# A graph network layer on one core: the residual of its output added by the store's DMA

## The chip, the cores and the metric

The kernel runs on one core of a Trainium2 chip. The metric is the device time of one execution in microseconds (us), the lower the better. It is given as the median of several executions; the profile is of one further execution.

## What is computed

The layer takes x, 32 graphs (batches) of 512 nodes with 256 features, and adj, their 512 x 512 adjacency matrices of zeros and ones, all in 32-bit floats. Cut to what matters:

```python
h = max(layernorm(x), 0)
conv  = relu(bn2(conv17(relu(bn1(conv1(h))))) + h)       # along the nodes
s     = h @ w_se.T + b_se
A     = exp(-|s_n - s_m|^2) * adj
nmp   = A @ relu(h @ w_msg.T + b_msg)
gi, gh = [conv, nmp] @ w_ih.T + b_ih,  h @ w_hh.T + b_hh
r, z  = sigmoid(gi_r + gh_r), sigmoid(gi_z + gh_z)
n     = tanh(gi_n + r * gh_n)
out   = x + (1 - z) * n + z * h
```

The change concerns the `x +` of the last line.

## The kernel before

**Layout.** Most of the work is done turned: features on the 128 partitions (two halves, `o` = 0 and 1), the 512 nodes of one batch along the free dimension. The result of one batch and one half is called an output block here: a tile of 128 x 512. There are 64 of them. The output in DRAM has nodes as rows, so a block has to be turned. VectorE's transpose turns pieces of 32 x 32, and the DMA places the pieces: `OB` and `XB` are views of the output and of x whose rows are nodes in 16 groups of 32. One block is moved by four DMAs of 64 KB, one for each group of 32 partitions, in pieces of 128 bytes (32 floats) in DRAM.

**Streams and plan.** The program is one long straight line of instructions without a loop on the chip. A planner written out in Python orders it when it is built. It keeps a clock `now` for TensorE and, for VectorE and ScalarE, the time at which each will be free (`dve.free`, `act.free`), from a cost for each instruction. Five streams take turns by due times: rows (first convolution), begins (layer norm and turning), graphs (messages and adjacency), conv (the 17 taps, as products in a transformed form), gates (what makes the output). `later(t, f)` puts work off to time t of the plan, and background work (sums, operands, weights) is added whenever VectorE's planned work ends soon. So a VectorE instruction more or less changes the places of later ones on all engines.

**Queues.** SP issues the loads in program order: weights `w` (L571), hidden rows `hT`, `hTg`, `hTb` (L211, L218, L225), `xconv` (L232), `xnb` (L252), adjacency (L340), turned inputs and residuals (`blocks`, L958). GpSimd (POOL) issues the stores: `hd` (L170, L993), `nd` (L170), `cd` (L721), `wd` (L583), `xd` (L979) and the output (L1140). Each of these instructions waits in its queue until its data or buffer is ready, and those behind it wait too. Several of the loads read what one of the stores wrote to DRAM.

**The output.** `gates(b)` runs over both halves. `reset` (L1151) and `update` (L1181) make the two gates on ScalarE, `mix_next` (L1095) the tanh, and then VectorE works off a block: in `mix_last` (L1102) `o_sb<-hTb,r`, `o_sb<-z,o_sb` and `r<-o_sb,r`, in `leave` (L1117) the transpose `o_sb<-r` and the addition `res<-o_sb,res`. `store` (L1136) writes `res` out with four DMAs on POOL. `load_res` (L963) loads the block of x, in the same turned-piece form, into one of two `res` buffers; `store` calls it for the block two later as soon as its own DMAs are issued, so these loads wait on SP for the store to free the buffer. The very last block (batch 31, half 1; `is_last`) is handled in two pieces along the nodes, with `mix_ahead` (L1126) doing what doesn't need the tanh earlier, and with its stores on the SP and ScalarE queues.

Of the kernel before, what the change touches and what calls it, by code (L numbers as in the profile page):

```python
# [8 lines left out]
F32 = mybir.dt.float32  # L9
AF = mybir.ActivationFunctionType  # L10
ALU = mybir.AluOpType
PSUM = bass.MemoryType.PSUM

P = 128
# [18 lines left out]
U = 29  # L33
Q = 18
# [15 lines left out]
def kernel(  # L50
# [31 lines left out]
    nc = tc.nc  # L82
    B, N, D = x.shape
# [19 lines left out]
    late = None  # L103
# [27 lines left out]
    dve, act = Engine(nc.vector, 0.12, 0.00108), Engine(nc.scalar, 0.16, 0.0009)  # L131

    def matmul(ps, lhsT, rhs, **more):
        nonlocal now
        now += max(0.223, 0.005 + elements(ps) / 600.0)
        nc.tensor.matmul(ps, lhsT, rhs, **more)  # L136
# [21 lines left out]
    def later(t, f):  # L158
        LATER.append((t, f))
        LATER.sort(key=lambda e: e[0])  # L160

    def settle():
        while LATER:
            LATER.pop(0)[1]()
# [14 lines left out]
    def settle_stores():  # L179
        while STORES:  # L180
            STORES.pop(0)()


    XS, HT, HB, HR, HR_AT, HG, XN, XR = {}, {}, {}, {}, {}, {}, {}, {}
# [35 lines left out]
    def load_gates(b):  # L220
        if b >= B or b in HB:
            return
        settle_stores()
        HB[b] = late.tile([P, ND, N], F32, name="hTb", bufs=2)
        nc.sync.dma_start(HB[b], HD[b])  # L225
        HB_AT[b] = now + 8.0
# [21 lines left out]
    def load_sums(b, d):  # L248
        if b < B and (b, d) not in XN:
            settle_stores()  # L250
            XN[b, d] = late.tile([P, N], F32, name="xnb", bufs=2)
            nc.sync.dma_start(XN[b, d], ND_[b, d])  # L252
# [700 lines left out]
    OB = out.rearrange("b (k i) d -> b i k d", i=32)  # L953

    def blocks(t, rows, o):
        for g in range(P // 32):
            at = o * P + 32 * g
            nc.sync.dma_start(  # L958
                t[32 * g : 32 * g + 32, :].rearrange("i (k j) -> i k j", j=32),
                rows[:, :, at : at + 32],  # L960
            )

    def load_res(b, o):  # L963
        if b < B and (b, o) not in XR:
            XR[b, o] = late.tile([P, N], F32, name="res", bufs=2)
            blocks(XR[b, o], XB[b], o)


# [91 lines left out]
    def gates(b):  # L1060

        nonlocal gating
        load_gates(b)
        gating = b
        load_sums(b, 0)
        load_sums(b, 1)
        if b == 0:
# [32 lines left out]
            later(act.free + 0.3, lambda: mix_last(r, z, o, s))  # L1100

        def mix_last(r, z, o, s):  # L1102
            load_res(b, o)
            y = XR[b, o]
            if is_last(o):
                dve.tensor_tensor(z[:, s], z[:, s], r[:, s], op=ALU.mult)
                dve.transpose(r[:, s], z[:, s])
                dve.tensor_tensor(y[:, s], r[:, s], y[:, s], op=ALU.add)
                later(dve.free + 0.4, lambda: store(y, o, s))
                return  # L1110
            t = late.tile([P, N], F32, name="o_sb")
            dve.tensor_tensor(t, hT[:, o, :], r, op=ALU.subtract)
            dve.scalar_tensor_tensor(t, z, 1.0, t, op0=ALU.add, op1=ALU.mult)
            dve.scalar_tensor_tensor(r, t, 0.5, r, op0=ALU.mult, op1=ALU.add)
            later(dve.free, lambda: leave(r, t, y, o))

        def leave(r, t, y, o):  # L1117

            dve.transpose(t, r)
            dve.tensor_tensor(y, t, y, op=ALU.add)  # L1120
            later(dve.free + 0.4, lambda: store(y, o, slice(0, N)))

        def is_last(o):
            return b == B - 1 and o == ND - 1
# [11 lines left out]
        def store(y, o, s):  # L1136
            for g in range(P // 32):
                at = slice(32 * g, 32 * g + 32)
                queue = nc.gpsimd if s.stop - s.start == N else nc.scalar if g % 2 else nc.sync
                queue.dma_start(  # L1140
                    OB[b][:, s.start // 32 : s.stop // 32, o * P + 32 * g : o * P + 32 * g + 32],
                    y[at, s].rearrange("i (k j) -> i k j", j=32),
                )
            if s.stop == N:
                del XR[b, o]
                load_res(b + o, 1 - o)

        for o in range(ND):
            r = z = None

            def reset():  # L1151
                nonlocal r
                settle()
                if b == 0:
                    load_res(b, o)
                r = late.tile([P, N], F32, name="r", bufs=2)
                act.activation(r, ps_r, AF.Tanh, bias=brz[:, o : o + 1], scale=0.5)

            def hidden_half(ps_h, s=slice(0, N)):
                act.activation(  # L1160
                    ps_h[:, s], ps_h[:, s], AF.Identity, bias=bn[:, o : o + 1], scale=0.5
                )

            halves = []

            hidden_at = 0.0

            def reset_hidden():
                nonlocal hidden_at
                while halves:  # L1170
                    ps, s = halves.pop(0)
                    dve.scalar_tensor_tensor(
                        ps[:, s], r[:, s], 1.0, ps[:, s], op0=ALU.add, op1=ALU.mult
                    )
                    hidden_at = dve.free + 0.3

            def reset_later(ps_h, s=slice(0, N)):
                halves.append((ps_h, s))
                later(act.free + 0.3, reset_hidden)

            def update():  # L1181
                nonlocal z
                z = late.tile([P, N], F32, name="z")
                act.activation(
                    z, ps_z, AF.Tanh, bias=brz[:, ND + o : ND + o + 1], scale=0.5
                )

            def mix(ps_n, s=slice(0, N)):
                later(now + 0.3, lambda r=r, z=z, o=o: mix_next(r, ps_n, z, o, s))

            ps_r = acc.tile([P, N], F32, name="ps_acc")
            ps_h = None
            yield from products(ps_r, o, 0, (0,), of=(0, 2))
            if o == 0:
                ps_h = acc.tile([P, N], F32, name="ps_acc")
                yield from products(ps_h, o, 2, (0,), lambda: hidden_half(ps_h))
                yield lambda: RES.get(b, 1e9) < 1e9
                yield RES[b]
                x_in.extend([XC[b][:, i, :] for i in range(ND)] + [XN[b, d] for d in range(ND)])
            yield from products(ps_r, o, 0, (1, 2), reset, (0, 2))  # L1200

            if ps_h is None and not is_last(o):
                ps_h = acc.tile([P, N], F32, name="ps_acc")
                yield from products(ps_h, o, 2, (0,), lambda: hidden_half(ps_h))
            if ps_h is not None:
                reset_later(ps_h)
            else:
                parts = []
                for s in (slice(0, N - P), slice(N - P, N)):
                    ps = acc.tile([P, N], F32, name="ps_acc")  # L1210
                    parts.append((ps, s))
                    for i in range(ND):
                        matmul(
                            ps[:, s], whh[:, i, cols(o, 2)], hT[:, i, s],
                            start=(i == 0), stop=(i == ND - 1), skip_group_check=True,
                        )
                    hidden_half(ps, s)
                    reset_later(ps, s)
                    yield now
            ps_z = acc.tile([P, N], F32, name="ps_acc")  # L1220
            yield from products(ps_z, o, 1, (0, 1, 2), update)
            if o == 0:
                load_gates(b + 1)
            if not is_last(o):
                reset_hidden()
                yield hidden_at
                yield from products(
                    ps_h, o, 2, (1, 2) if o == 0 else (2, 1), lambda: mix(ps_h), clear=False
                )
                continue  # L1230

            later(act.free + 0.2, lambda: mix_ahead(z, o))
            for ps, s in parts:
                for j in range(2 * ND):
                    matmul(
                        ps[:, s], wih[:, j, cols(o, 2)], x_in[j][:, s],
                        start=False, stop=(j == 2 * ND - 1), skip_group_check=True,
                    )
                mix(ps, s)
                yield now  # L1240
            settle()
# [109 lines left out]
    while 0 in NORMS:  # L1351
# [8 lines left out]
        op=ALU.add,  # L1360
# [10 lines left out]
    for b in (2, 3):  # L1371
        at = (b - 2) * NT * D
# [10 lines left out]
    while streams:  # L1383
# [10 lines left out]
        name = min(able, key=lambda k: clock[k])  # L1394
# [64 lines left out]
```

## Time and profile before

| | |
|---|---|
| median of 3 executions | 2083.01 us (2079.53 to 2084.8) |
| the profiled execution, and its span | 2089.1 us, 2087.2 us |
| first and last residual addition on VectorE | 303.9 us, 2082.7 us |
| loads of res on SP | 256 of 64 KB, median 4.1 us from issue to landing |
| stores of res on POOL | 252 of 64 KB, 649 ns each at the median, 2.8 us to landing |
| DMA packets | 545,861, of which 456,512 are under 512 bytes |
| HBM read and written | 278.55 MB and 98.04 MB |

The span runs from the first to the last instruction of the program in the profiled execution. Busy times of an engine are unions of its instructions. A group line gives the source line, the engine, the operation, what it writes and reads, and the count. A wait line gives the waiting engine and instruction, what released it, the sum in us, how many waits there were, and the longest. L127, L136 and L141 are lines of helpers through which nearly all VectorE, ScalarE and TensorE work is recorded, so groups are told apart by their tiles.

### The profile page before, as it was taken

The numbers are of one execution on the slowest core, as the hardware profiler recorded it, in microseconds if no ns is written. First come the engines' busy times: TensorE is split into PE (matmuls) and PEld (weight loads), VectorE is DVE, ScalarE is ACT, GpSimd is POOL, SyncE is SP. The second block draws the span as 40 slices with busy tenths as digits, with TensorE's granted clock in tenths as the row PEclk, the third lists the DMA queues.
The fourth block names the chain that finished last, engine by engine and source line by source line (L and its number), as shares of the span: only waits on it lengthen the run. The fifth ranks groups of instructions, "written<-read, shape, count | busy, mean of one in ns | idle before, by whom it ended". The sixth has DMA issues, their size and how long they took to land.

```text
span 2087.2 us, 25989 instructions
## 1 busy us (share of the span) xinstructions
PE 2053.2 (98%) x8724; PEld 1260.0 (60%) x8724; DVE 1364.5 (65%) x2441; ACT 827.7 (40%) x1585; POOL 337.4 (16%) x578
## 2 busy tenths in 40 slices
PE   9999999999999999999999999999999999999998
PEld 5888566666566565665666665456655666644444
DVE  6789677866778566875677764577774668643223
ACT  5544653333633346234353343533333533332221
POOL 2100121221211112111121111311110210021111
PEclk9999999999999999999999999999999999999999
DMA  7455778777877767786678775778674666434342
GB/s 281 151 176 187 237 227 220 200 197 203 238 193 206 205 174 214 201 212 160 188 220 216 187 193 155 197 188 222 177 202 145 185 175 163 145 95 106 73 96 41
DMA packets 545861, 378.36 MB, mean 181 GB/s; under 512 B 456512, under 2 KB 473440, under 8 KB 545088
## 3 DMA queue, kind: packets, MB, share of 16 engines
q1 hardware_dynamic: 512848, 278.76, 50.8%
q0 software_dynamic: 28192, 84.70, 12.6%
q10 hardware_dynamic: 4688, 13.24, 1.7%
q8 instruction: 70, 1.15, 0.2%
q14 instruction: 63, 0.52, 0.1%
HBM read 278.55 MB, written 98.04 MB: 180 GB/s over the span
## 4 chain that ended last, share of the span: by engine, by line
PE 93%; DVE 3%; ACT 2%; DMA 1%; issue 1%; POOL 0%; SPq 0%; ACTq 0%; DVEq 0%
PE ps_acc L136 47%; PE ps_c L136 22%; PE ps_g L136 21%; PE ps_g L141 1%; PE ps_c L917 1%; DVE z L127 1%; DMA xconv<-cd 0%; PE ps_acc L146 0%; DVE st L127 0%; ACT h L127 0%; PE ps_g L917 0%; DVE x L127 0%; ACT y L127 0%; ACT x_sb L127 0%; DVE at L127 0%
## 5 line engine op out<-in xcount | busy, mean ns | idle before, releaser
L136 PE MATMUL ps_acc<-xconv,wih 128*128 128x512 f32 (+1 forms) x772 | 365.0, 595 | 0.0
L136 PE MATMUL ps_acc<-xnb,wih 128*128 128x512 f32 (+1 forms) x772 | 360.2, 592 | 0.0
L136 PE MATMUL ps_acc<-hTb,whh 128*128 128x512 f32 (+1 forms) x772 | 356.0, 590 | 0.0
L136 PEld LDWEIGHTS ps_c<-xd,w 128*128 128x128 f32 x2304 | 289.0, 191 | 64.2 <-issue 58.6
L136 PEld LDWEIGHTS ps_c<-x,w 128*128 128x128 f32 x2032 | 258.2, 192 | 89.8 <-issue 64.6
L136 PE MATMUL ps_c<-xd,w 128*128 128x135 f32 (+1 forms) x2304 | 291.5, 279 | 0.2
L136 PE MATMUL ps_c<-x,w 128*128 128x135 f32 (+2 forms) x2032 | 268.0, 281 | 11.0 <-ACT z L127 4.4
L1140 POOL DMA_DIRECT2D out_dram<-res x252 | 164.1, 657 | 704.5 <-DVE res L127 580.8
L136 PEld LDWEIGHTS ps_acc<-xconv,wih 128*128 128x128 f32 x772 | 142.5, 192 | 146.3 <-issue 143.7
L136 PE MATMUL ps_g<-at,msg 128*128 128x512 f32 x512 | 227.6, 593 | 1.3 <-DVE at L127 1.3
L136 PEld LDWEIGHTS ps_acc<-xnb,wih 128*128 128x128 f32 x772 | 141.4, 191 | 143.0 <-issue 140.8
L136 PEld LDWEIGHTS ps_acc<-hTb,whh 128*128 128x128 f32 x772 | 140.6, 190 | 142.4 <-issue 140.6
L127 DVE TENSOR_TENSOR msg<-ps_g,bmsg 128x256 f32<-128x256 f32 x128 | 53.9, 421 | 206.8 <-PE ps_g L136 206.6
L127 DVE TENSOR_TENSOR o_sb<-hTb,r 128x512 f32<-128x512 f32 x63 | 43.4, 690 | 202.4 <-ACT r L127 202.4
L136 PEld LDWEIGHTS ps_g<-at,msg 128*128 128x128 f32 x512 | 94.5, 190 | 106.1 <-issue 100.0
L127 DVE SCALAR_TENSOR_TENSOR x<-x,x 128x544 f32<-128x544 f32 (+5 forms) x161 | 137.6, 855 | 2.9
L127 DVE TENSOR_TENSOR x<-x 128x272 f32<-128x272 f32 (+5 forms) x280 | 127.0, 497 | 0.3
L136 PE MATMUL ps_g<-hT,w 128*128 128x512 f32 (+8 forms) x296 | 119.4, 550 | 2.8 <-ACT h L127 2.8
L127 DVE TENSOR_TENSOR xd<-x 128x544 f32<-128x544 f32 (+1 forms) x144 | 102.8, 718 | 29.1 <-PE ps_c L136 29.0
L127 ACT ACTIVATE ps_c<-ps_c 128x270 f32<-128x270 f32 (+1 forms) x144 | 56.3, 391 | 165.1 <-PE ps_c L136 165.1
L136 PE MATMUL ps_g<-wmsg,hTg 128*128 128x259 f32 x496 | 121.6, 381 | 0.0
L127 ACT ACTIVATE z<-ps_acc,brz 128x512 f32<-128x512 f32 x64 | 43.9, 686 | 188.8 <-PE ps_acc L136 188.8
(125 smaller groups left out, 2343.7 us busy)
## 6 DMA issues: line engine op xcount, KB each, us to landing
w<-wd SPq DMA_DIRECT2D x120, 768.0 KB, 5.7
m_sb<-in_adj_dram SPq DMA_DIRECT2D x384, 64.0 KB, 3.5
hT<-hd SPq DMA_DIRECT2D x33, 512.0 KB, 4.7
hd<-hT POOLq DMA_DIRECT2D x32, 512.0 KB, 6.1
hTb<-hd SPq DMA_DIRECT2D x32, 512.0 KB, 5.6
xnb<-nd SPq DMA_DIRECT2D x64, 256.0 KB, 3.2
res<-in_x_dram SPq DMA_DIRECT2D x256, 64.0 KB, 4.1
out_dram<-res POOLq DMA_DIRECT2D x252, 64.0 KB, 2.9
```

Source lines behind the costliest of these rows:

```text
L127: getattr(self.engine, name)(*tiles, **more)
L136: nc.tensor.matmul(ps, lhsT, rhs, **more)
L141: nc.tensor.transpose(ps, a, ident)
L917: nc.tensor.matmul(pss[c], gr.left[k, :], gr.right[k, :], start=True, stop=True, tile_position=(32 * c, 0),)
L1140: queue.dma_start(OB[b][:, s.start // 32 : s.stop // 32, o * P + 32 * g : o * P + 32 * g + 32], y[at, s].rearrange("i (k j) -> i k j", j=32),)
```

## The change

At the start of `gates(b)` a DMA copies the batch's x from DRAM to the output in DRAM (for batch 31 only the first half of the features). The stores of a block, which stay on POOL, no longer write a finished sum: they add the turned block to what the output holds. `o_sb`, which holds the turned block, is stored directly and gets two buffers. The residual tiles, their loads and the addition on VectorE are gone for all blocks but the last. The last block still loads its x, now in `reset` of that block and into a buffer of the pool `part`, and still stores plainly through SP and ScalarE.

```diff
     def load_res(b, o):
-        if b < B and (b, o) not in XR:
-            XR[b, o] = late.tile([P, N], F32, name="res", bufs=2)
+        if (b, o) not in XR:
+            XR[b, o] = late.tile([P, Q * U], F32, name="part", bufs=3)[:, :N]
             blocks(XR[b, o], XB[b], o)
...
         load_gates(b)
         gating = b
+        if b < B - 1:
+            nc.sync.dma_start(out[b], x[b])
+        else:
+            nc.sync.dma_start(out[b][:, :P], x[b][:, :P])
         load_sums(b, 0)
         load_sums(b, 1)
...
         def mix_last(r, z, o, s):
-            load_res(b, o)
-            y = XR[b, o]
             if is_last(o):
+                y = XR[b, o]
                 dve.tensor_tensor(z[:, s], z[:, s], r[:, s], op=ALU.mult)
...
-            t = late.tile([P, N], F32, name="o_sb")
+            t = late.tile([P, N], F32, name="o_sb", bufs=2)
             dve.tensor_tensor(t, hT[:, o, :], r, op=ALU.subtract)
             dve.scalar_tensor_tensor(t, z, 1.0, t, op0=ALU.add, op1=ALU.mult)
             dve.scalar_tensor_tensor(r, t, 0.5, r, op0=ALU.mult, op1=ALU.add)
-            later(dve.free, lambda: leave(r, t, y, o))
+            later(dve.free, lambda: leave(r, t, o))
 
-        def leave(r, t, y, o):
+        def leave(r, t, o):
 
             dve.transpose(t, r)
-            dve.tensor_tensor(y, t, y, op=ALU.add)
-            later(dve.free + 0.4, lambda: store(y, o, slice(0, N)))
+            later(dve.free + 0.4, lambda: store(t, o, slice(0, N)))
...
         def store(y, o, s):
             for g in range(P // 32):
                 at = slice(32 * g, 32 * g + 32)
-                queue = nc.gpsimd if s.stop - s.start == N else nc.scalar if g % 2 else nc.sync
-                queue.dma_start(
-                    OB[b][:, s.start // 32 : s.stop // 32, o * P + 32 * g : o * P + 32 * g + 32],
-                    y[at, s].rearrange("i (k j) -> i k j", j=32),
-                )
-            if s.stop == N:
-                del XR[b, o]
-                load_res(b + o, 1 - o)
+                dst = OB[b][:, s.start // 32 : s.stop // 32, o * P + 32 * g : o * P + 32 * g + 32]
+                src = y[at, s].rearrange("i (k j) -> i k j", j=32)
+                if is_last(o):
+                    (nc.scalar if g % 2 else nc.sync).dma_start(dst, src)
+                else:
+                    nc.gpsimd.dma_start(dst, src, accum_op=ALU.add)
...
             def reset():
                 nonlocal r
                 settle()
-                if b == 0:
+                if is_last(o):
                     load_res(b, o)
```

The adding stores wait on POOL for the copy of their batch. In the built program the four stores of a block are the same four DMAs as before, with an addition.

## The prediction

> **What bounds the kernel now.** I read the page's busy times first, then a table of busy time by stretch (the columns of each row are the stretch, its length, and the busy time of PE, PEld, DVE, ACT and POOL with instruction counts, then the granted clock, the DMA share and GB/s), then the chain that ended last.
>
> ```profile
> span 2087.2 us, 25989 instructions
> PE 2053.2 (98%) x8724; PEld 1260.0 (60%) x8724; DVE 1364.5 (65%) x2441; ACT 827.7 (40%) x1585; POOL 337.4 (16%) x578
> ...
> PE 93%; DVE 3%; ACT 2%; DMA 1%; issue 1%; POOL 0%; SPq 0%; ACTq 0%; DVEq 0%
> ```
>
> ```profile
> 0.00:300.00 300.00, 288.23 (x1693) 218.97 (x1694) 225.15 (x490) 155.20 (x301) 40.50 (x82) 0.98 0.63 214
> 300.00:900.00 600.00, 590.21 (x2560) 367.01 (x2559) 433.20 (x770) 249.28 (x493) 108.00 (x179) 0.99 0.74 202
> 900.00:1500.00 600.00, 599.71 (x2441) 357.75 (x2440) 405.42 (x716) 238.01 (x462) 102.27 (x170) 1.00 0.73 193
> 1500.00:1842.00 342.00, 336.46 (x1468) 209.54 (x1468) 216.55 (x352) 124.18 (x248) 41.86 (x76) 0.99 0.60 166
> 1842.00:2088.00 246.00, 238.59 (x568) 106.76 (x566) 84.14 (x115) 61.07 (x84) 44.80 (x71) 0.99 0.37 84
> ```
>
> TensorE is the bound in every stretch. Its idle time is 11.8 us before 300, then 9.8, 0.3 and 5.5, and 7.4 in the last stretch: 34.8 us. The first output block is made at 304 us, so before 300 only the plan can move; the 7.4 us at the end are the last block's chain, which the change leaves. What the change can win by lighter VectorE or DMA work is at most 9.8 + 0.3 + 5.5 = 15.6 us, 0.75%.
>
> Busy time could hide slack, since matmuls overlap. So I looked at how often they start: two 128x512 matmuls of the gates start 0.43 us apart throughout, and from 1842 to 2077 us the chain of waits holds nothing but them, 552 in 235.2 us, or 0.426 each. There is no hidden slack there.
>
> Where does VectorE or a DMA hold TensorE up? The largest case near an output block is at 1804 us, in VectorE's timeline (start, length, instruction) and the waits of that stretch:
>
> ```profile
> 1799.49 0.70 DVE L127 STREAM_TRANSPOSE o_sb<-r 128x512 f32<-128x512 f32 x1
> 1800.23 0.69 DVE L127 TENSOR_TENSOR res<-o_sb,res 128x512 f32<-128x512 f32 x1
> ...
> 1803.49 0.72 DVE L127 SCALAR_TENSOR_TENSOR z<-n 128x540 f32<-128x540 f32 x1
> ```
>
> ```profile
> PE ps_c L136 <- ACT n L127: 1.2, 1, 1.2
> ```
>
> The addition that the change removes stood ahead of the convolution's sums, ScalarE waited for those, and TensorE lost 1.2 us.
>
> The DMA side, with the waits of POOL and of SP's queue:
>
> ```profile
> q1 hardware_dynamic: 512848, 278.76, 50.8%
> q0 software_dynamic: 28192, 84.70, 12.6%
> ```
>
> ```profile
> POOL out_dram L1140 <- DVE res L127: 580.8, 44, 34.8
> ...
> SPq L958 <- DMA out_dram<-res: 58.1, 17, 8.4
> ```
>
> The queues fill 65% of sixteen engines, and POOL mostly waits for data to store.
>
> **What the Trainium skill says.** "Perfetto Trace Analysis", Identifying the Most-Contended Engine, calls matmul busy share a bad measure of headroom; hence the 0.43 us above, which here agrees with the busy share. "DMA: Bandwidth & Descriptors", SWDGE vs HWDGE vs iDMA, says that only GpSimd can issue an accumulating DMA; the plain stores are there already, so no queue changes. The same page, Rules for kernel authors, says that an accumulate reads its destination and writes it later, and must wait for an earlier writer's semaphore; the built program has that wait. "Collectives: The Full Stack", The bandwidth ceiling, says that the addition costs by its two reads, not by adding. No run here shows an accumulating DMA.
>
> **The change, part by part.** All against the profiled execution: 2089.1 us, 1.9 of them around the span. The median is 2083.0, so 6.1 come off at the end.
>
> *Residual additions gone.* 63 x 0.692 = 43.6 us of VectorE's 1364.5, 3.2%. Only what is on the chain counts: additions into res are 2.2 us of it, and about 1.5 of those (0.6% of the last 246 us) are in the last block and stay. So 0.7 us, plus perhaps 0.3 elsewhere where such an addition stands in front of a sum: -1.
>
> *Residual loads gone.* 252 of 256 DMAs of 64 KB leave SP: at a median of 0.487 us, some 120 us of its issuing, and 58.1 us in which SP stood waiting for a store to free res (17 times), with weights and hidden rows queued behind. The chain names one such load (4.2 us to landing at 1798.2), but VectorE was then busy until 1798.9 with the addition of xconv, so its worth is near 0, at most 4.2. I take -1 for SP running ahead. On the engines, 252 x 512 = 129,024 pieces of 128 bytes go; the trace's packet records give 13.8 ns for one, so 1.78 of the 33.4 ms of sixteen engines, 5.3%.
>
> *Copies added.* 32 on SP, all but the last of 512 KB, no waits of substance, each ahead of its batch's xnb loads or soon behind them: 0.5 us of SP's time a batch. Such a load lands in 3.2 us, and the last xnb loads, issued at 2047.1, were first read at 2059.8. A DRAM to DRAM copy is not in the trace; at the 4096-byte packet's 195 ns its 16.8 MB take 0.80 ms, 2.4% (bounds: the same bytes at twice that, 4.8%; not below 0). The first adding store of a batch comes at least half of a batch, 15.4 us, after its copy; a 512 KB load lands in 4 to 6. I cost the copies at 0.
>
> *Stores that add.* 252 on POOL, as many as before, 0.657 us each, ready 0.7 us earlier. The first of a batch waits for the copy too (landed, above); behind it on POOL stand the stores of nd, hd and cd that SP's loads wait for. Its price is the unknown. From below: POOL's time unchanged, landing 2.9 us. From above: POOL's time doubled, and each 128-byte piece handled alone. If the read comes as 129,024 more pieces of 13.8 ns, engines gain 5.3% of load, which cancels the loads removed. I take landing 4 to 8 us and POOL unchanged, because two reads for one explain no more: 0 on the path. The ends are priced under the rivals.
>
> *A new wait.* o_sb is now read by a DMA and has two buffers, so VectorE's first instruction of a block (o_sb<-hTb,r) waits for the stores of two blocks earlier; all of VectorE is behind it in order. Two blocks are 30.9 us at the fastest pace (36 matmul pairs of 0.858), the store leaves some 4 us after its buffer is taken: about 26 us of cover, so 0.
>
> *The last block.* Its residual now goes into a part buffer, loaded behind the last xnb loads, as before at about 2048.5; it is used at 2079.7. The four adding stores before it were issued by 2072.3, and the final stores start at 2083.6: eleven us of cover before landing counts. 0.
>
> *The plan.* The order is made by a planner that counts VectorE's time; with 43 us less, the instructions from the second output block on stand elsewhere (the built orders differ on every engine, with the same matmuls). This could give or take some of the 15.6 us: 0, bounds -8 and +9.
>
> Sum: -1 - 1 = -2, so 2087 in the profiled execution's terms, 2081 in the median's.
>
> **The rivals.** *A, no change that can be told (0.3%, 6.2 us, is about what this measurement can tell):* 2081, own range 2077 to 2087. For it: PE at 99 to 100% where the blocks are made.
>
> *B, faster:* the lighter VectorE and SP remove half of the 15.6 us: 2083 - 8 = 2075; all of it, 2067. For it: the stall at 1804, SP's 58 us. Against: most stalls end with ScalarE behind convolution products, not with res.
>
> *C, slower, POOL as the new delay:* an accumulating DMA costs POOL 1.3 us instead of 0.65, or lands late, so that nd, hd and cd stores behind a group of four come 2.6 us or more later. hidden rows are planned 8 us after their load and land in 4.7 to 5.6, so it decides from about 2.5 to 3 us of lateness, that is from 1.3 us of POOL for one. If two of three of the 49 blocks before 1842 then cost TensorE 0.6 us: +20, 2103. For it: hT loads already waited for hd (32.9 us in 6 waits). Against: POOL is 16% busy.
>
> *D, slower by the plan alone:* stalls grow by 9 us: 2092.
>
> *E, slower, pieces added one after the other:* a block's four stores are 128 pieces for each of 16 engines, so from 26 / 128 = 0.2 us a piece the new o_sb wait ends last. The skill's DMA page (Latency and other measured facts) puts one HBM access at 0.2 us on average; read and write in turn would be about 0.4, an estimate: 51 us a block where the fast stretch has 15.4 and the rest 31.5. That is 15 x 36 + 49 x 20 = 1500 us more; at 0.25 us, 32 us a block, about 250 more, 2330.
>
> **How the numbers follow.** A 0.38, B 0.22, C 0.22, D 0.10, E 0.08. Faster by over 0.3% is B, 0.22; within it A, 0.38; slower C, D and E, 0.40. The time is A's, 2081. The range runs from 2070, leaving out the best of B (0.04), to 2112, leaving out E and the worst of C (0.16).
>
> **What would show it.** Right: 32 copies and no res on SP but the last block's; VectorE some 44 us lighter; POOL's L1146 near 0.65 us each; landings under 10 us; PE idle from 300 to 1842 near 15 us; no long o_sb wait for a DMA. Wrong: L1146 at 1.3 us or more with nd, hd or hT waits grown (C); o_sb waiting for out_dram (E); the same DMA figures but other TensorE stalls (B or D).

## The result, and the profile after

The changed kernel takes 2068.57 us (median of four, 2064.94 to 2070.59), the kernel before beside it 2083.91: a ratio of 0.9913, 95% interval 0.9892 to 0.9934. It is 0.9% faster. The forecast was no change that can be told, 2081 us, with a range from 2070; the measured time lies just below that range, where the prediction had put rival B (2075, at best 2067). The profiled executions have spans of 2087.2 and 2068.8 us.

From the page of the changed kernel, the span and busy times, the two large DMA queues, and the group of the adding stores (busy us and mean ns of one, then the idle time before them and what ended it):

```profile
span 2068.8 us, 25327 instructions
PE 2046.3 (99%) x8724; PEld 1256.4 (61%) x8724; DVE 1319.8 (64%) x2378; ACT 827.0 (40%) x1585; POOL 451.7 (22%) x578
...
q1 hardware_dynamic: 381312, 278.74, 47.9%
q0 software_dynamic: 153184, 84.70, 23.9%
...
L1146 POOL DMA_DIRECT2D out_dram<-o_sb x252 | 276.6, 1733 | 522.1 <-DVE o_sb L127 512.6
```

VectorE lost the 44 us that it was to lose. POOL did not keep its price: an adding store costs it 1.73 us, not 0.65, and its queue's share of the DMA engines nearly doubled, from 12.6 to 23.9%. By the page alone, this looks like rival C. And yet the kernel is faster.

Where the time went shows in the table by stretch (stretch, length, busy PE, PEld, DVE, ACT and POOL, the granted clock, which is the share of its full clock at which TensorE was let run, the DMA engines' busy share, GB/s). The last stretch, in which TensorE works on nothing but the gates, begins near 1825 us now and began at 1842 before:

```profile
300.00:900.00 600.00, 596.39 (x2608) 371.38 (x2608) 426.90 (x764) 253.56 (x503) 140.89 (x182) 0.99 0.82 204
900.00:1500.00 600.00, 599.71 (x2476) 360.17 (x2475) 395.59 (x700) 237.64 (x464) 140.24 (x171) 1.00 0.82 195
1500.00:1825.00 325.00, 325.00 (x1399) 200.08 (x1398) 208.42 (x336) 121.37 (x241) 59.02 (x75) 1.00 0.69 168
```

TensorE's idle time from 300 us to the last stretch went from 15.6 to 3.6 + 0.3 + 0 = 3.9 us: 11.7 us of the 18.4 by which the two profiled spans differ. Nearly all of the rest is in TensorE's busy time: the same 8724 matmuls took 2053.2 us before and 2046.3 now, at a mean granted clock of 0.990 and 0.994. First the idle time. TensorE's own waits in that part, of the kernel before and then of the changed one (what waited for what: us in total, times, longest):

```profile
PE ps_c L136 <- ACT z L127: 4.4, 1, 4.4
PE ps_c L136 <- ACT at L127: 3.2, 1, 3.2
PE ps_g L136 <- ACT h L127: 2.8, 1, 2.8
PE ps_c L136 <- ACT n L127: 2.3, 2, 1.2
PE ps_c L917 <- ACT z L127: 1.6, 2, 1.4
PE ps_g L917 <- ACT h L127: 1.3, 2, 1.0
```

```profile
PE ps_g L917 <- ACT h L127: 1.3, 2, 1.0
PE ps_c L136 <- ACT n L127: 1.1, 1, 1.1
PE ps_c L136 <- ACT z L127: 0.8, 1, 0.8
PE ps_c L136 <- ACT ps_c L127: 0.4, 1, 0.4
PE ps_c L917 <- ACT z L127: 0.2, 1, 0.2
```

Few waits are concerned: three single ones of 4.4, 3.2 and 2.8 us are most of the difference. None of them names the residual.

Now the busy time. A pause can cost more than its length. This is TensorE's timeline of the kernel before at its longest one:

```profile
1563.21 2.17 PE L136 MATMUL ps_c<-x,w 128*128 128x135 f32 x8 [4.37 <-ACT z L127]
1565.17 3.49 PE L136 MATMUL ps_acc<-xconv,wih 128*128 128x512 f32 x4
```

Four such matmuls take 1.88 us elsewhere; after the pause they took 3.49, and the granted clock of the 25 us from 1550 was 0.86. For the 25 us from 700 and from 815, around the other two long pauses, it was 0.94 and 0.93; in the changed kernel it was 1.00 in all three. The Trainium skill ("TensorE: Matmul & The Clock Gate", Part 1: The HAM clock gate) says that the clock halves after an idle window of about 3.4 us. The longest pause agrees with that, but in this execution the slow clock also followed on the pauses of 3.2 and 2.8 us, which are shorter.

Nor does it follow each time. Below is the pause of 2.8 us in the kernel before, and then in e2, a kernel from the next section in which TensorE has the same order and the same waits:

```profile
721.82 5.40 PE L136 MATMUL ps_g<-hT,w 128*128 128x512 f32 x8 [2.78 <-ACT h L127]
```

```profile
716.15 3.70 PE L136 MATMUL ps_g<-hT,w 128*128 128x512 f32 x8 [2.78 <-ACT h L127]
```

So the slow clock's share differs between executions of one order, and 6.9 us holds for these two profiles alone. The medians differ by 15.3 us; taking off the 11.7 us of idle time leaves some 4 us for the slow clock, an estimate.

### The profile page after: what moved, and what is told of

Its sections match the earlier page's. It is cut to its first block, busy times and chain, and to the rows that moved or that the text cites. A ratio compares the mean times of both kernels' runs of the same rounds, so it can differ in the third digit from the quotient of the medians.

```text
span 2068.8 us, 25327 instructions
## 1 busy us (share of the span) xinstructions
PE 2046.3 (99%) x8724; PEld 1256.4 (61%) x8724; DVE 1319.8 (64%) x2378; ACT 827.0 (40%) x1585; POOL 451.7 (22%) x578
## 3 DMA queue, kind: packets, MB, share of 16 engines
q0 software_dynamic: 153184, 84.70, 23.9%
## 4 chain that ended last, share of the span: by engine, by line
PE 61%; DVE 1%; issue 1%; DMA 0%; POOL 0%; ACT 0%; DVEq 0%; POOLq 0%; ACTq 0%
PE ps_acc L136 36%; PE ps_c L136 13%; PE ps_g L136 10%; PE ps_c L917 1%; PE ps_g L141 0%; DMA cd<-part 0%; DVE y L127 0%; POOL cd L721 0%; DVE part L127 0%; ACT part L127 0%; DVE o_sb L127 0%; DVE right L127 0%; DVE x L127 0%; POOL out_dram L1146 0%; PE ps_g L917 0%
## 5 line engine op out<-in xcount | busy, mean ns | idle before, releaser
L1146 POOL DMA_DIRECT2D out_dram<-o_sb x252 | 276.6, 1733 | 522.1 <-DVE o_sb L127 512.6
```

The costliest lines, as they stand in the source:

```text
L1146: nc.gpsimd.dma_start(dst, src, accum_op=ALU.add)
```

## The experiments

Three readings stood against each other: the new order of instructions alone (P), VectorE's lighter load (V), and SP freed of loads and of waits for their buffers (Q). The planner counts VectorE's time, so the change always moves the order too. But what an instruction costs and what the planner counts for it can be set apart: `nc.vector` issues without counting, and adding to `dve.free` counts without issuing. In all of e1 to e6 TensorE's instructions stand, by tile and shape, exactly either as before or as in the changed kernel, while VectorE's load and the DMAs differ.

**e1: the old kernel, its addition not counted.** TensorE's new order, all of the old work.

```diff
-            dve.tensor_tensor(y, t, y, op=ALU.add)
+            nc.vector.tensor_tensor(y, t, y, op=ALU.add)
```

> The kernel before, with its residual loads, its addition on VectorE and its plain stores, but the planner no longer counts the addition's time. TensorE's instructions then stand in exactly the order of the changed kernel. Theory P (the gain comes from the new order alone): 2066 to 2072 us, TensorE idle from 300 us to the tail about 4 us. Theory V (lighter VectorE): as before, 2081 to 2087. Theory Q (SP freed of the residual loads and of the waits for their buffers): as before, 2081 to 2087.

**e2: the changed kernel, a dead addition counted and made.** TensorE's old order, with copies, adding stores and no residual loads.

```diff
             dve.transpose(t, r)
+            dve.tensor_tensor(late.tile([P, N], F32, name="extra"), t, t, op=ALU.add)
             later(dve.free + 0.4, lambda: store(t, o, slice(0, N)))
```

> The changed kernel, with an addition of the same size put back on VectorE into a tile that nobody reads, and counted by the planner. TensorE's order is exactly that of the kernel before. Theory P: 2081 to 2087 us. Theory V: 2081 to 2087. Theory Q: 2066 to 2072, since loads and store waits stay away.

**e3: the changed kernel, an addition counted and not made.**

```diff
             dve.transpose(t, r)
+            dve.free += dve.fixed + dve.each * N
             later(dve.free + 0.4, lambda: store(t, o, slice(0, N)))
```

> The changed kernel, with the planner counting an addition that isn't made: the order of the kernel before without its VectorE work, without its loads. Theory P: 2081 to 2087 us. Theory V: 2066 to 2072. Theory Q: 2066 to 2072.

**e4: the changed kernel, a dead addition made and not counted.**

```diff
             dve.transpose(t, r)
+            nc.vector.tensor_tensor(late.tile([P, N], F32, name="extra"), t, t, op=ALU.add)
             later(dve.free + 0.4, lambda: store(t, o, slice(0, N)))
```

> The changed kernel in its own order, with an addition of 128x512 put back on VectorE (into a tile that nobody reads) that the planner doesn't count: 43.6 us more of VectorE. Theory P: 2066 to 2072 us. Theory V: 2081 to 2087. Theory Q: 2066 to 2072.

These four ran on one chip, beside the kernel before at 2087.39 us:

| kernel | TensorE's order | addition on VectorE | residual | median us | ratio to before (95%) |
|---|---|---|---|---|---|
| e1 | new | yes | loads, plain stores | 2070.46 | 0.9920 (0.9900 to 0.9940) |
| e4 | new | yes | copies, adding stores | 2071.01 | 0.9921 (0.9900 to 0.9941) |
| e2 | old | yes | copies, adding stores | 2085.27 | 0.9998 (0.9986 to 1.0010) |
| e3 | old | no | copies, adding stores | 2085.99 | 0.9994 (0.9981 to 1.0007) |

P holds in all four, V and Q fail: V in e1, e3 and e4, Q in e1, e2 and e3. The old kernel with its residual loads, its addition and its plain stores is as fast as the changed one when it gets the new order (e1). And everything that the change does to DMAs and queues together, in the old order, is worth 0.02%, with an interval of 0.12% (2.5 us) to either side (e2).

The stalls tell the same. TensorE's waits from 300 to 1842 us in e2, then in e3, which does not even make the addition:

```profile
PE ps_c L136 <- ACT z L127: 4.4, 1, 4.4
PE ps_c L136 <- ACT at L127: 3.2, 1, 3.2
PE ps_g L136 <- ACT h L127: 2.8, 1, 2.8
PE ps_c L136 <- ACT n L127: 2.3, 2, 1.2
```

```profile
PE ps_c L136 <- ACT z L127: 4.4, 1, 4.4
PE ps_c L136 <- ACT at L127: 3.2, 1, 3.2
PE ps_g L136 <- ACT h L127: 2.8, 1, 2.8
PE ps_c L917 <- ACT z L127: 1.6, 2, 1.4
PE ps_c L136 <- ACT n L127: 1.5, 2, 1.1
```

Other DMAs, another load of VectorE, and the same pauses to a tenth of a microsecond. Of these lines one differs in e3: without the addition `ACT n` has 1.5 us instead of 2.3. The stall at 1804 us, which the prediction had picked as its example, makes the difference: it is 1.2 us in the kernel before and in e2, and this in e3:

```profile
PE ps_c L136 <- ACT n L127: 0.4, 1, 0.4
```

That part of the mechanism is real, and it is worth 0.8 us. The executions profiled for e2 and e3 have TensorE busy for 2046.1 and 2047.7 us, as the changed kernel has: what sets these two apart from the changed kernel's profile is idle time, almost alone.

**e5: do the adding stores cost anything?** The changed kernel with plain stores. It leaves out the residual of all blocks but the last; the copies stay.

```diff
-                    nc.gpsimd.dma_start(dst, src, accum_op=ALU.add)
+                    nc.gpsimd.dma_start(dst, src)
```

> The changed kernel with plain stores on POOL instead of adding ones (left out: the residual of all blocks but the last; the copies stay). Same order. If the adding stores cost something on the path: below 2064 us. If POOL's 1.73 us for each and the landing of 5.0 us are hidden: 2064 to 2072, with POOL back at about 0.65 us each and its 450 us of busy time down by some 110 us (the first reading: the order alone decides).

2067.98 us, ratio 0.9899 (0.9878 to 0.9920), not to be told from the changed kernel's 0.9913. The stores by tile (ns of one, lowest, median, highest), of the changed kernel and of e5:

```profile
L1146 POOL DMA_DIRECT2D out_dram<-o_sb x252: 1052/1619/2437, 305.4 to 2052.8; - x126
```

```profile
L1146 POOL DMA_DIRECT2D out_dram<-o_sb x252: 649/649/717, 303.9 to 2050.8; - x126
```

POOL's busy time fell from 452 to 337 us and q0's share from 23.9 to 12.6%. So the whole of that extra work is the addition's, and within the intervals it is hidden.

Rival C had a chain in mind: late stores of the hidden rows `hd`, then late loads `hT` on SP. SP's queue waited for `hd` at these loads for 32.9 us in 6 waits before; in the changed kernel and then in e5:

```profile
SPq L211 <- DMA hd<-hT: 58.7, 7, 13.1
```

```profile
SPq L211 <- DMA hd<-hT: 58.9, 7, 12.9
```

The wait is as long with plain stores, and it is 56.1 us in e1, so most of its growth comes with the order. In the old order the adding stores go with 47.8 us (e2), and the time doesn't change.

**e6: what makes the old order's stalls?** In the old order two of them have the same picture. From e3, VectorE near 713 us, then near 1552, and the waits of the second place (brackets: idle time before an instruction, and what ended it):

```profile
712.86 0.71 DVE L127 STREAM_TRANSPOSE hT<-x_sb 128x512 f32<-128x512 f32 x1 [9.72 <-PE ps_g L136]
```

```profile
1547.78 0.69 DVE L127 SCALAR_TENSOR_TENSOR r<-o_sb,r 128x512 f32<-128x512 f32 x1
1552.83 0.71 DVE L127 STREAM_TRANSPOSE hT<-x_sb 128x512 f32<-128x512 f32 x1 [4.36 <-PE ps_g L136]
1553.47 0.67 DVE L127 STREAM_TRANSPOSE right<-m_sb 128x512 f32<-128x512 f32 x1
1554.17 0.69 DVE L127 TENSOR_TENSOR at<-right,at 128x512 f32<-128x512 f32 x1
1554.78 1.84 DVE L127 TENSOR_TENSOR y<-y,z 128x1620 f32<-128x1620 f32 x1
```

```profile
ACT z L127 <- DVE y L127: 10.4, 1, 10.4
...
PE ps_c L136 <- ACT z L127: 4.4, 1, 4.4
```

At the second place VectorE stood 4.36 us at a transpose that needs a buffer `hT`, which TensorE was still reading for the convolution's rows. The sum y<-y,z stood behind it in order, ScalarE waited for that, and TensorE for ScalarE. At the first place VectorE stood 9.72 us, and TensorE lost 2.8. In e6 the turned rows get a buffer of their own (the 2 KB a partition of each of the old `res` tiles are free in the changed kernel), in the otherwise unchanged e3:

```diff
-            HT[b] = front.tile([P, ND, N], F32, name="hT", bufs=2)
+            HT[b] = (
+                front.tile([P, ND, N], F32, name="hT", bufs=2) if late is None
+                else late.tile([P, ND, N], F32, name="hTt", bufs=1)
+            )
```

> As e3 (order of the kernel before, no addition, no residual loads), but the turned hidden rows of begin(b) go to a buffer of their own instead of one shared with the loaded rows of the convolution, so that VectorE's transposes hT<-x_sb no longer wait for TensorE to have read the other rows. TensorE's order is unchanged. Theory H (two of the old order's stalls, 2.9 us near 714 and 4.5 us near 1552, come from this wait at the head of VectorE's queue): both go, and with the slow clock after them 7 to 10 us: 2075 to 2079. Rival S (ScalarE's and VectorE's other work at those places makes the stalls whatever frees the transposes): stalls stay within 1 us, 2084 to 2088.

2076.84 us, ratio 0.9946 (0.9928 to 0.9965), against e3's 0.9994: about 10 us, at the upper end of what H expects, and outside S's range. In e6 VectorE goes through both places without a pause at the transpose (shown for the second), and of TensorE's waits the ones of 4.4 and 2.8 us are gone:

```profile
1544.94 0.69 DVE L127 SCALAR_TENSOR_TENSOR r<-o_sb,r 128x512 f32<-128x512 f32 x1
1545.55 0.70 DVE L127 STREAM_TRANSPOSE hTt<-x_sb 128x512 f32<-128x512 f32 x1
...
1547.49 1.84 DVE L127 TENSOR_TENSOR y<-y,z 128x1620 f32<-128x1620 f32 x1
```

```profile
PE ps_c L136 <- ACT at L127: 3.2, 1, 3.2
PE ps_c L917 <- ACT z L127: 1.6, 2, 1.4
PE ps_c L136 <- ACT n L127: 1.5, 2, 1.1
```

So about half of what separates the two orders is this one head-of-queue wait, in two places: e6 is 0.54% ahead of the kernel before, and e7, below, the new order measured beside it, 1.01%. The rest wasn't tried by itself: the 3.2 us at 827, where three ScalarE copies y<-z of 1.5 us each stand ahead of what TensorE waits for, and the smaller ones.

**e7: the same buffer in the changed kernel.** The edit of e6.

> The changed kernel with the same buffer of its own for the turned hidden rows. It has no TensorE stall behind these transposes, so both theories expect the changed kernel's time, 2064 to 2071.

2067.09 us, ratio 0.9899 (0.9879 to 0.9919): the changed kernel's time, as expected.

**e8 to e11: is the new order good, or was the old one bad?** The kernel before, with nothing but a constant of the planner's cost of VectorE changed. e8:

```diff
-    dve, act = Engine(nc.vector, 0.12, 0.00108), Engine(nc.scalar, 0.16, 0.0009)
+    dve, act = Engine(nc.vector, 0.11, 0.00108), Engine(nc.scalar, 0.16, 0.0009)
```

> The kernel before with nothing changed but one constant of the planner: an instruction of VectorE is counted with 0.11 us of fixed time instead of 0.12. All instructions are the same, in another order. If the order of before is an ordinary draw: TensorE stalls of 4 to 25 us from 300 us to the tail, 2066 to 2094. If the new order is better for a reason that has to do with the addition alone, this one stays at 2081 to 2088.

e9, e10 and e11 have 0.13, 0.10, and 0.12 with 0.00112 for an element.

> The kernel before with VectorE's fixed cost counted as 0.13 us instead of 0.12, nothing else. If orders near the old one scatter (its stalls are accidents of places): anywhere from 2064 to 2094 us, and TensorE's stalls from 300 us to the tail at other places than in before. If most orders are like that of before: 2081 to 2090.

> The kernel before with the fixed cost counted as 0.10 us. Scatter: 2064 to 2094 us. Most orders like that of before: 2081 to 2090.

> The kernel before with VectorE's cost for an element counted as 0.00112 us instead of 0.00108. Scatter: 2064 to 2094 us. Most orders like that of before: 2081 to 2090.

| kernel before with | median us | ratio to before (95%) |
|---|---|---|
| 0.11 (e8) | 2066.25 | 0.9900 (0.9877 to 0.9924) |
| 0.13 (e9) | 2070.14 | 0.9919 (0.9904 to 0.9934) |
| 0.10 (e10) | 2069.15 | 0.9912 (0.9896 to 0.9927) |
| 0.00112 (e11) | 2070.82 | 0.9918 (0.9904 to 0.9933) |

All four take the changed kernel's time, without the change. The orders differ from before and from each other, but the outcome does not scatter over the width that I had allowed: the four ratios lie within 0.2% of one another, and of the orders measured here only that of before is 1% off. The expectation that most orders would be like before is wrong for each, and so is the picture of a broad scatter. Their waits are other ones; those of e8 from 300 to 1842 us:

```profile
PE ps_c L136 <- ACT z L127: 2.3, 1, 2.3
PE ps_g L917 <- ACT h L127: 1.3, 2, 1.0
PE ps_c L917 <- ACT right L127: 0.9, 1, 0.9
```

**e12: both at once.** The changed kernel with e6's buffer and e8's constant.

> The changed kernel with the buffer of its own for the turned hidden rows and the fixed cost counted as 0.11 us, as in e8. If what is left to win between 300 us and the tail is the idle time of some 4 us and a good order is no better than another: 2062 to 2070 us, not beyond e7's and e8's intervals. An unlucky draw: above 2072.

2068.35 us, ratio 0.9911 (0.9895 to 0.9928). The two gains do not add up: once the long pauses are gone, the idle time from 300 to 1825 us is 3 to 6 us in every order measured. No version here is faster than the changed kernel by more than the intervals. Why all these orders, with waits at different places, come to the same idle time was not tried.

## Why the prediction was wrong

- *What bounds the kernel, and how much is to be had:* right in kind. TensorE is the bound; the gain is its idle time between 300 us and the tail. The ceiling of 15.6 us was read too low, since it counted idle time only. Gate matmuls do not start 0.43 us apart throughout: four took 3.49 us instead of 1.88 after the longest pause. That slow clock was 6.9 us of the difference between the two profiles, and some 4 of that between the medians.
- *Residual additions gone, -1:* not contradicted. The stall at 1804 us is 0.8 us shorter in e3, and e3 is not to be told from e2 by time.
- *Residual loads gone, -1:* 0 within the interval of e2, which cannot tell 1 us. SP's 58 us of waiting for stores did vanish, and TensorE's waits stayed.
- *Copies at 0:* right. One lands in 6.0 us at the median, and the 31 of 512 KB took 0.71 ms of the engines' time by the packet records, for 0.80 estimated for all.
- *Stores that add, at 0:* right on the path within the intervals of e2 and e5, wrong in itself. I took POOL's time as unchanged; it is 2.7 times as long, beyond the 1.3 us at which rival C was to decide. Landing was 5.0 us, inside 4 to 8. I took landing and POOL's time from two reads for one, and the price is not that (last section). C's threshold was wrong too: POOL passed it, and in the old order (e2) the time stayed. Its sign, longer waits of hT loads for hd, did come, but e1 and e5 have it with plain stores: most of it belongs to the order.
- *The new wait and the last block at 0:* right; no o_sb instruction of VectorE waited for a store, and the last block's first store starts 2.2 us after TensorE's last group of matmuls starts, as before.
- *The plan at 0, bounds -8 and +9:* this is the step that failed. It is the whole of the result as far as can be told: e1 gives -0.80%, 16.9 us, by the order alone, twice the bound of -8, and e2 -0.02% by all the rest. I treated the order as noise around zero. But the profile of before had shown three pauses of 2.8 to 4.4 us, of which e6 traces two to one wait for a buffer, and none of which names the residual. A change of order could lose such pauses more easily than repeat them; that was a guess from the profile, and e8 to e11 bear it out for this kernel. The right number for this term was not 0 but -15 to -17 us.

Rival B's time was nearest, but its reason, a lighter VectorE and SP, fell with e1 to e4; had it been chosen, the hit would have been luck. Rival D had the right cause and the wrong sign.

## What to carry to other kernels

Where a planner or scheduler turns costs into an order, a change has two effects, that of its work and that of the new order; undo the one without the other (count without issuing, issue without counting) before crediting the work. Before a forecast, list the bound engine's longest single waits and ask of each whether it belongs to what is changed or to where things happen to stand: if they are few, long and unrelated to it, a new order alone may gain, as five did here (e1 and e8 to e11). And where one order is slower than its neighbours, moving a constant of the planner can mend it, without any change to the work.

## What the runs showed of the hardware

- An adding store from GpSimd costs POOL 1.05 to 2.44 us for 64 KB in pieces of 128 bytes, where the plain one costs 0.65. Its packets are single pieces: 129,024 packets of 128 bytes at a mean of 39 ns in the packet records, where the plain stores of e5 went in packets of 4096 bytes; the queue has 153,184 packets with the addition and 28,192 without. From issue to landing it took 5.0 us, and 3.3 with plain stores in the same order (e5). The Trainium skill ("Collectives: The Full Stack", The bandwidth ceiling) puts the cost of an addition in a collective down to its two reads. Here the adding packets took 5.05 ms of the DMA engines' time; the 4032 packets of 4096 bytes that they replace would take some 0.8 ms at e5's mean of 198 ns, an estimate. Two reads alone do not explain that; what does was not tried.
- Pauses repeat, the slow clock after them does not: the same three long waits of TensorE came out alike to 0.1 us in three kernels with the same order and different DMA traffic, but the eight matmuls behind the wait of 2.78 us took 5.40 us in one and 3.70 in another.
